# Vector products through SBUF, a third PSUM bank for background work, and one GpSimd instruction for two scan results

## The chip, the core and the metric

The kernel runs on one core of a Trainium2 chip. A core has a matrix engine (TensorE: PE, its weight loads PEld), a vector engine (VectorE: DVE), a scalar engine (ScalarE: ACT), a general engine (GpSimd: POOL) and a queue processor (SyncE: SP) that here issues every DMA. Each engine runs its own instructions in their order and waits on semaphores for the others. Data lie in HBM, in SBUF (128 partitions, the working memory) and in PSUM (128 partitions of eight 2 KB banks), which the matrix engine writes.

The metric is the device time of one execution in microseconds: 11066.59 as the median of three (11065.08 to 11072.03).

## What is computed

Two layers on `x` of shape (8, 96, 64, 64). Layer 0 is a state space block (normalization, a projection, a 3x3 depthwise convolution, a selective scan in four directions, a gate) followed by a small convolutional block with channel attention; layer 1 is linear attention and an 8-bit feed-forward. Nearly all of the time is in the selective scan of layer 0:

```python
delta = softplus(dts + dt_bias)
h0 = zeros((b, K, D_INNER, D_STATE))          # K = 4 directions, 192 channels, 16 states

def step(h, inp):                             # over L = 4096 positions
    u_t, d_t, b_t, c_t = inp
    dA = exp(d_t[..., None] * A)
    h = dA * h + (d_t * u_t)[..., None] * b_t[:, :, None, :]
    y = einsum('bkdn,bkn->bkd', h, c_t)
    return (h, y)
```

For each of 8 images, 4 directions, 192 channels and 16 states a first-order recurrence runs over 4096 positions; the states are then weighted with `c_t` and summed.

## The kernel before

**Tiling of the scan.** Images go in 4 pairs `p`. The 2 x 192 channels of a pair fill three blocks `T` of 128 rows. Positions go in 4 chunks `ci` of 1024 columns. One (p, k, ci, T) is a job; there are 192 (`jobs`, before the main loop at L1400). In a job a tile of 128 partitions holds 32 channels x 4 states; `j` counts the four groups of channels and `q` the four groups of states. One (job, j, q) is a unit of 128 x 1024 numbers, 3072 in all. The main loop takes two units a turn, so it has 1536 pairs.

**One pair, by engine.**
- PE: `spread(g)` (L1299) copies 32 rows of `du` (delta times input) to 128 partitions, into the PSUM tile `pu` (2 banks), once for every four units (a group `g`).
- ACT: `decay(u)` (L1304) makes `da` = exp(A delta) in SBUF, four buffers.
- VectorE: `scan(u)` (L1311). First two products `pb[i]` = `pu` x `bm` (`bm` is B of the recurrence, loaded in SBUF); then two scans `hc` = scan(`da`, `pb[i]`), which start from `carry` but in the first chunk. In this text the products are P0 and P1, the scans S0 and S1, in this order. Both `pbs` are PSUM tiles of two banks each (L437); `hc` is in SBUF, 8 buffers of one unit (L426).
- GpSimd: in the same function, for each of the two units, a copy of the last column into `carry` (not in the last chunk, `ci` = 3) and the product `hc` = `hc` x `cm` (`cm` is C of the recurrence). Its four instructions stand in the order copy, product, copy, product, each copy waiting for its own scan.
- PE and ACT: `total(g-1)` (L1349) sums four units of the group before over states into the PSUM tile `yp`; ACT copies the sum to `y` and SP stores it, some with a read-back of the sum of another direction (`prev`, `yet`).
- SP: `weights` (L1268) loads `bm` and `cm` ahead (4 and 5 buffers), `fetch` loads `dl`. A `cm` or `bm` tile belongs to a (q, batch) and is used for two or four `j`.

**Order on the engines.** `pe`, `ve`, `se`, `ge` are recorders of the class `InOrder` (L254): each engine's instructions are chained in the order in which the program writes them, so every one of them has line 266 in the profile. A tile scheduler orders only the DMAs by their own waits.

**Background work.** All that isn't the scan (the convolutions and projections of the next pair of images, the gate and the second block of the last one, `du` and `dls` of the next job through `steps`, L467) is written as Python generators, "lanes", that a planner of class `Slots` (L283) steps twice a pair: `slots.run()` once before `scan(u)` and once after it. A lane that needs PSUM calls `take` (L301): it gets bank `pg` on even slots or `yp` on odd ones (`yp` is also `total`'s) where the bank is free and where two running budgets of PE and ACT time, filled at RATE a slot up to CAP, are positive; `long` asks hold `pg` over several slots. `give` (L321) frees a bank one slot later. PSUM is full: `pg` 1 + `yp` 1 + `pu` 2 + two `pbs` 4 = 8 banks. Background work on GpSimd (products `u`, `du`, `turn`, `acc`, `tn`) stands between the `hc` products in its order.

After the loop a tail (`tp`, `tps` pools) finishes the last pair of images; ahead of it phase A does the first.

Of the kernel before, what the change touches and what calls it, by code (L numbers as in the profile page):

```python
# [9 lines left out]
F32 = mybir.dt.float32  # L10
F16 = mybir.dt.float16
BF16 = mybir.dt.bfloat16
F8 = mybir.dt.float8e5
AF = mybir.ActivationFunctionType
ALU = mybir.AluOpType
# [4 lines left out]
B, C, H, W = 8, 96, 64, 64  # L20
# [7 lines left out]
CH = 1024  # L28
NCH = L // CH
# [253 lines left out]
class Slots:  # L283
# [4 lines left out]

    RATE, CAP = (2.0, 1.8), (3.0, 2.4)

    def __init__(self, *banks):
        self.lanes, self.later, self.first, self.at, self.due = [], [], None, 0, {}
        self.banks, self.held, self.big = banks, set(), set()
        self.left, self.behind = [0.0, 0.0], lambda: False

    def pay(self, *times):
        self.left = [v - t for v, t in zip(self.left, times)]

    def take(self, pe, act, long=0):  # L301
        while True:
            i = 1 if self.at % 2 and not long else 0


            due = long and (
                self.at % 4 > (long == 2) or self.at % 16 <= 6 < self.at % 16 + long
            )
            if i not in self.held and not due and min(self.left) > (-2 if long else 0):
                self.held.add(i)  # L310
                self.pay(pe, act)
                return self.banks[i]
            yield

    def take_big(self, *which):
# [4 lines left out]

    def give(self, bank):  # L321
        i = self.banks.index(bank)
        self.after(1, lambda: self.held.remove(i))

    def after(self, n, f):
# [25 lines left out]
def phase_b(  # L351
# [7 lines left out]
    nc = tc.nc  # L359
    with ExitStack() as ctx:  # L360
# [25 lines left out]
        make_identity(nc, ident)  # L386
        eps = cp.tile([128, 1], F32, name="eps")
        nc.vector.memset(eps, EPS)
        gmean = cp.tile([C, C], F32, name="gmean")
        nc.vector.memset(gmean, 1.0 / (C * 128))  # L390
        mean96 = cp.tile([C, C], F32, name="mean96")
        nc.vector.memset(mean96, 1.0 / C)
        vec = load("vec96", [C, 10])
# [29 lines left out]
        inner = ExitStack()  # L423
        bcp = inner.enter_context(tc.tile_pool(name="b_bc", bufs=4))
        wp = inner.enter_context(tc.tile_pool(name="b_w", bufs=2))
        hp = inner.enter_context(tc.tile_pool(name="b_h", bufs=8))  # L426
        gp = inner.enter_context(tc.tile_pool(name="b_bg", bufs=1))
        psc = inner.enter_context(tc.tile_pool(name="b_ps", bufs=1, space=PSUM))

# [4 lines left out]
        yps = psc.tile([128, 512], F32, name="yp")  # L434
        bank0 = psc.tile([128, 512], F32, name="pg")
        pu = psc.tile([128, CH], F32, name="pu")
        pbs = [psc.tile([128, CH], F32, name=f"pb{i}") for i in range(2)]  # L437
        pe = InOrder(tc, nc.tensor, mybir.EngineType.PE)
        ve = InOrder(tc, nc.vector, mybir.EngineType.DVE)
        se = InOrder(tc, nc.scalar, mybir.EngineType.Activation)  # L440
        ge = InOrder(tc, nc.gpsimd, mybir.EngineType.Pool)
        halves = [slice(h * 512, h * 512 + 512) for h in range(CH // 512)]
        slots = Slots(bank0, yps)

        jobs = [
            (p, k, ci, T) for p in range(NP) for k in ((1, 3, 0, 2) if p else (0, 2, 1, 3))
            for ci in range(NCH) for T in (0, 2, 1)
        ]
        units = [(job, j, q) for job in range(len(jobs)) for j in range(4) for q in range(4)]
        carries, bcs, dus, dls, sts, das, hcs, prevs, yet = ({} for _ in range(9))  # L450
        turned, resting, squeezed_at = set(), set(), set()

        def where(job):
# [4 lines left out]
        def batch(u):  # L458
            job, j, q = units[u]
            T = jobs[job][3]  # L460
            return j // 2 if T == 2 else T
# [5 lines left out]
        def steps(job):  # L467

            p, k, ci, c, T, at = where(job)
            if T == 0:  # L470

                sts[job // 3] = gp.tile([32 + 2 * R, 512], F32, name="st")
                r0 = 64 + R * (k // 2)
                for i, hs in enumerate(halves):
                    for b in range(2):
                        nc.sync.dma_start(
                            sts[job // 3][32 * i + R * b : 32 * i + R * b + R, :],
                            xd_d[k % 2][2 * p + b][r0 : r0 + R, at][:, hs],
                        )
            dtw = gp.tile([32 + 2 * R, 128], F32, name="dtw")  # L480
            for i in range(2):
                nc.sync.dma_start(dtw[32 * i : 32 * i + 2 * R, :], a["dtw"][:, k, T, :])
            dus[job] = gp.tile([128, CH], F32, name="du", bufs=2)
            nc.sync.dma_start(dus[job], xi_d[k % 2][p][T][:, at])
            yield

            while slots.at % 16 != 6:
                yield
            dl = gp.tile([128, CH], F32, name="dls")
            for i, hs in enumerate(halves):  # L490
                bank = slots.banks[i]
                assert i not in slots.held
                slots.held.add(i)
                slots.pay(0.9, 2.5)
                rows = slice(32 * i, 32 * i + 2 * R)
                pe.matmul(bank, dtw[rows, :], sts[job // 3][rows, :], start=True, stop=True)
                se.activation(dl[:, hs], bank, AF.Softplus, bias=dtb[:, k, T : T + 1])
                slots.give(bank)
                if i:
                    exps()  # L500
                else:
                    yield
            ge.tensor_mul(dus[job], dus[job], dl)
            yield from wait(2)
            nc.sync.dma_start(dl_d[k][p][T][:, at], dl)
            yield
# [243 lines left out]
        def rest(b, s):  # L750
# [139 lines left out]
            for j in range(8):  # L890
# [14 lines left out]
                x8 = gp.tile([C, 512], F8, name=f"x8{s}")  # L905
                se.copy(x8, xc, saturate=False)
                yield
                h8 = gp.tile([128, 3, 512], F8, name=f"h8{s}")

                def cast(o, t):  # L910
                    return lambda: se.copy(o, t, saturate=False)
# [1 line left out]
                for i in range(3):  # L913
                    bank = yield from slots.take(0.3, 1.3)
                    pe.matmul(bank, w1q[:, i * 128 : i * 128 + 128], x8, start=True, stop=True)
                    h16 = gp.tile([128, 512], F16, name=f"h16{s}")
                    se.copy(h16, bank)
                    se.activation(h16, h16, AF.Relu, bias=b1f[:, i : i + 1])
                    slots.give(bank)
                    slots.after(1, cast(h8[:, i, :], h16))  # L920
                    yield
                yield from wait(1)
                bank = yield from slots.take(0.7, 1.3)
                for i in range(3):
                    pe.matmul(
                        bank[0:C, :], w2q[:, i, :], h8[:, i, :], start=(i == 0), stop=(i == 2)
                    )
                o16 = gp.tile([128, 512], F16, name=f"h16{s}")[0:C, :]
                se.copy(o16, bank[0:C, :])
                se.activation(o16, o16, AF.Identity, bias=b2f)  # L930
                slots.give(bank)
# [85 lines left out]
        def before_scans(p):  # L1017
# [26 lines left out]
            def norms(b):  # L1044
# [16 lines left out]
                for j in js:  # L1061
# [13 lines left out]
                    if j < 7:  # L1075
                        nxt = fetch(j + 1)
                    bank = yield from slots.take(0.1, 2.5)
                    pe.matmul(bank[0:C, 0:4], gmean, cs, start=True, stop=True)
                    se.mul(ngm, bank[0:C, 0:4], -1.0)
                    slots.give(bank)  # L1080
                    sq = u(5)[0:C, 0:512]
                    for i, q in enumerate(quarters):
# [3 lines left out]
                        )  # L1086
                    yield
                    bank = yield from slots.take(0.1, 0.5)
                    pe.matmul(bank[0:C, 0:4], gmean, gs, start=True, stop=True)
                    se.activation(r, bank[0:C, 0:4], AF.Ln, bias=eps[0:C])  # L1090
                    se.activation(r, r, AF.Exp, scale=-0.5)
                    slots.give(bank)
                    slots.after(1, times(ngm, r))
# [174 lines left out]
        def weights(u, i):  # L1268

            if u >= len(units):  # L1270
                return
            job, j, q = units[u]
            p, k, ci, c, T, at = where(job)
            b = batch(u)
            if (job // 3, b, q, i) in bcs:
                return
            t = bcp.tile([128, CH], F32, name=("bm", "cm")[i], bufs=(4, 5)[i])
            r0 = 32 * (k // 2) + 16 * i + 4 * q
            nc.sync.dma_start(
                t, xd_d[k % 2][2 * p + b][r0 : r0 + 4, at].unsqueeze(0).to_broadcast([32, 4, CH])  # L1280
            )
            bcs[job // 3, b, q, i] = t

# [27 lines left out]
        def scan(u):  # L1311

            job, j, q = units[u]
            p, k, ci, c, T, at = where(job)
            step, last = (-1, 0) if k >= 2 else (1, CH - 1)
            for i in range(2):
                ve.tensor_mul(pbs[i], pu, bcs[job // 3, batch(u), q + i, 0])
            for i in range(2):
                t = hp.tile([128, CH], F32, name="hc")
                carry = carries[p, k][:, T, 4 * j + q + i : 4 * j + q + i + 1]  # L1320
                ve.tensor_tensor_scan(
                    t[:, ::step], das.pop(u + i)[:, ::step], (pbs[i])[:, ::step],
                    0.0 if ci == 0 else carry, ALU.mult, ALU.add,
                )
                hcs[u + i] = t
            for i in range(2):
                v = u + i
                carry = carries[p, k][:, T, 4 * j + q + i : 4 * j + q + i + 1]
                if ci < NCH - 1:
                    ge.tensor_copy(carry, hcs[v][:, last : last + 1])  # L1330
                ge.tensor_mul(hcs[v], hcs[v], bcs[job // 3, batch(u), q + i, 1])

        def before(g):

# [14 lines left out]
        def total(g):  # L1349
# [9 lines left out]
            for n in range(4):  # L1359
                for i in range(4):  # L1360
                    pe.matmul(
                        yp[32 * i : 32 * i + 32, :], add,
                        hcs[4 * g + n][:, 256 * i : 256 * i + 256],
                        start=(n == 0 and k < 2), stop=(n == 3),
                    )
            for n in range(4):
                hcs.pop(4 * g + n)
            y = wp.tile([128, 256], F32, name="y")
            to = y_d if k == 2 else ys_d[1]
# [577 lines left out]
```

## Time and profile before

| | us |
|---|---|
| median of the runs | 11066.59 |
| the profiled execution's span | 11058.4 |
| first product of the loop starts | 214.57 |
| last scan pair of the loop (starts, lasts) | 10719.00, 4.57 |
| VectorE busy between them | 10318.6 |
| GpSimd busy between them | 8960.45 |
| ACT busy between them | 6404.01 |
| PE busy between them | 7459.47 |
| mean granted TensorE clock | 0.815 |

Other rows of the view by groups that the next sections use: GpSimd's products on 128 x 512 (`u<-u,u`, 180 of them) take 1271 ns on average, the `du` products on 128 x 1024 2358 ns, the `carry` copies 183 ns. VectorE's scans without `carry` take 2275 ns. In the tail VectorE's fused products on 96 x 512 take 742 ns with an operand in PSUM (`w<-t,c_vec,w`), 740 ns from SBUF (`v<-v,c_vec,w`) and 752 ns on 128 x 512 from SBUF (`tn<-tn,c_on,cb`).

How to read it: a line of groups has the line, the engine, the operation, output<-inputs by tile name, the shapes, the count, then busy time in us and the mean of one in ns, then the idle time of the engine just before such instructions and what ended most of it. A line of the timeline has start and duration in us; equal neighbours are merged, with xcount and their joint duration.

### The profile page before, as it was taken

The numbers are of one execution on the slowest core, as the hardware profiler recorded it, in microseconds if no ns is written. First come the engines' busy times: TensorE is split into PE (matmuls) and PEld (weight loads), VectorE is DVE, ScalarE is ACT, GpSimd is POOL, SyncE is SP. The second block draws the span as 40 slices with busy tenths as digits, with TensorE's granted clock in tenths as the row PEclk, the third lists the DMA queues.
The fourth block names the chain that finished last, engine by engine and source line by source line (L and its number), as shares of the span: only waits on it lengthen the run. The fifth ranks groups of instructions, "written<-read, shape, count | busy, mean of one in ns | idle before, by whom it ended". The sixth has DMA issues, their size and how long they took to land.

```text
span 11058.4 us, 128094 instructions
## 1 busy us (share of the span) xinstructions
PE 7887.2 (71%) x39468; PEld 3111.6 (28%) x39468; DVE 10525.7 (95%) x6651; ACT 6596.3 (60%) x9175; POOL 9028.7 (82%) x6649
## 2 busy tenths in 40 slices
PE   7755778655568887767777787776767776665778
PEld 3322333222223332223222332223322222222223
DVE  4999999999999999999999999999999999999974
ACT  2544765544567666556776656565776656665554
POOL 2788877787898888998888887899889888988860
PEclk8877888877788888878878888887878877777889
DMA  3445554454555555666545555566544555644551
GB/s 117 151 165 180 160 156 157 141 188 156 163 185 172 171 172 157 211 214 195 158 152 160 157 178 159 177 220 209 172 157 159 160 164 179 197 157 140 173 157 37
DMA packets 900188, 1834.20 MB, mean 166 GB/s; under 512 B 247965, under 2 KB 421214, under 8 KB 892462
## 3 DMA queue, kind: packets, MB, share of 16 engines
q1 hardware_dynamic: 899502, 1826.01, 52.8%
q8 instruction: 314, 5.14, 0.2%
q14 instruction: 372, 3.05, 0.1%
HBM read 1405.13 MB, written 420.42 MB: 165 GB/s over the span
## 4 chain that ended last, share of the span: by engine, by line
PE 32%; issue 29%; DVE 17%; POOL 11%; ACT 6%; DMA 4%; SPq 0%; DVEq 0%; POOLq 0%; ACTq 0%
PE pu L266 12%; PE yp L266 11%; DVE hc L266 11%; POOL hc L266 7%; PE pg L266 6%; DVE pb L266 5%; ACT u L266 2%; ACT da L266 2%; POOL u L266 2%; PE t L266 2%; PE ps L197 1%; DMA bm<-xd 1%; POOL turn L266 1%; POOL carry L266 1%; ACT L266 1%
## 5 line engine op out<-in xcount | busy, mean ns | idle before, releaser
L266 POOL TENSOR_TENSOR hc<-hc,cm 128x1024 f32<-128x1024 f32 x3072 | 7230.0, 2359 | 591.0 <-DVE hc L266 382.6
L266 DVE TENSOR_TENSOR_SCAN hc<-da,carry,pb 128x1024 f32<-128x1024 f32 x2304 | 5276.8, 2334 | 38.1 <-ACT da L266 31.5
L266 PE MATMUL pu<-du,c_sel 128*128 128x512 f32 x3072 | 2452.5, 944 | 2244.1 <-DVE pb L266 2239.6
L266 DVE TENSOR_TENSOR pb<-pu,bm 128x1024 f32<-128x1024 f32 x3072 | 3601.6, 1220 | 133.9 <-PE pu L266 105.9
L266 ACT ACTIVATE da<-dl,c_alog 128x1024 f32<-128x1024 f32 x3072 | 3352.8, 1140 | 91.4 <-DVE hc L266 73.8
L266 PEld LDWEIGHTS pu<-du,c_sel 128*128 128x128 f32 x3072 | 790.0, 281 | 3521.1 <-DVE pb L266 2784.8
L266 DVE TENSOR_TENSOR_SCAN hc<-da,pb 128x1024 f32<-128x1024 f32 x768 | 1713.1, 2275 | 38.9 <-ACT da L266 22.8
L266 ACT COPY y<-yp 128x256 f32<-128x256 f32 x768 | 284.4, 370 | 2348.9 <-PE yp L266 2198.4
L266 PE MATMUL yp<-hc,c_add 128*32 128x256 f32 x24576 | 1660.8, 416 | 22.6 <-ACT s L266 6.6
L266 PEld LDWEIGHTS yp<-hc,c_add 128*32 128x32 f32 x24576 | 768.6, 120 | 1200.1 <-issue 628.4
L266 POOL COPY carry<-hc 128x1 f32<-128x1 f32 x2304 | 422.5, 183 | 766.1 <-DVE hc L266 744.9
L266 ACT ACT_TABLE_LOAD x566 | 726.2, 1283 | 38.2 <-DMA cb<-zs 16.9
L266 ACT COPY u<-pg 128x512 f32<-128x512 f32 (+6 forms) x397 | 218.3, 550 | 712.3 <-PE pg L266 641.2
L266 POOL TENSOR_TENSOR u<-u,u 96x512 f32<-96x512 f32 (+1 forms) x426 | 537.5, 1269 | 105.9 <-ACT u L266 101.8
L266 POOL TENSOR_TENSOR du<-du,dls 128x1024 f32<-128x1024 f32 x192 | 452.7, 2358 | 91.5 <-ACT dls L266 91.1
L266 ACT COPY u<-yp 96x512 f32<-96x512 f32 (+6 forms) x347 | 188.0, 542 | 465.5 <-PE yp L266 404.5
L266 PE MATMUL pg<-ain,wmain 96*128 96x512 f32 x792 | 354.1, 599 | 0.0
L266 PE MATMUL pg<-ain,wmix 96*128 96x512 f32 x792 | 353.0, 598 | 0.0
L266 PE MATMUL yp<-prev,ident 128*128 128x256 f32 x768 | 321.9, 512 | 39.0 <-ACT u L266 27.4
L266 PEld LDWEIGHTS yp<-prev,ident 128*128 128x128 f32 x768 | 214.5, 283 | 381.8 <-issue 264.3
L266 PE MATMUL pg<-st,dtw 12*128 12x512 f32 x384 | 218.5, 649 | 49.4 <-ACT u L266 28.8
L266 PE MATMUL yp<-st,dtw 12*128 12x512 f32 x384 | 227.9, 674 | 18.3 <-ACT u L266 10.9
(340 smaller groups left out, 7030.2 us busy)
## 6 DMA issues: line engine op xcount, KB each, us to landing
dl<-dl SPq DMA_DIRECT2D x768, 512.0 KB
bm<-xd SPq DMA_DIRECT2D x512, 512.0 KB
cm<-xd SPq DMA_DIRECT2D x512, 512.0 KB
du<-xi SPq DMA_DIRECT2D x192, 512.0 KB
dl<-dls SPq DMA_DIRECT2D x192, 512.0 KB
ya<-y SPq DMA_DIRECT2D x384, 128.0 KB
prev<-ya SPq DMA_DIRECT2D x384, 128.0 KB
xi<-u SPq DMA_DIRECT2D x152, 256.0 KB
```

The source lines that it names most:

```text
L197: nc.tensor.matmul(bank[r, :].rearrange("p (h w) -> p h w", w=W), w[:, t if len(which) > 1 or w is wmix else 0, columns], pads[b][:, 8 * j ...
L266: op(*args, **kw)
```

## The change

1. `pbs[0]` becomes an SBUF tile; `pbs[1]` stays in PSUM. One of its two banks becomes `ph`, a bank for the lanes.
2. `hc` tiles and `cm` tiles are now two units wide (4 and 2 buffers of two units). One copy moves both carries of a pair, one GpSimd product of 128 x 2048 multiplies both units by C.
3. `Slots` has three banks. A lane takes the bank that rested longest; a `long` ask takes `ph`, else `pg`, and one at a time. RATE goes from (2.0, 1.8) to (2.2, 2.0) and CAP from (3.0, 2.4) to (4.0, 4.0).
4. `gmean` goes (`mean96` with a scale of 1/128 in the ACT instruction that follows), `h8` and `h16` share `u` tiles, and the scratch for descriptors that software makes is set to 1024.

```diff
-    RATE, CAP = (2.0, 1.8), (3.0, 2.4)
+    RATE, CAP = (2.2, 2.0), (4.0, 4.0)
...
+    def rested(self, i):
+        return i not in self.held and self.at > self.used[i] + 1
+    def hold(self, i):
+        self.held.add(i)
+        self.used[i] = self.at
     def take(self, pe, act, long=0):
         while True:
-            i = 1 if self.at % 2 and not long else 0
-            due = long and (
-                self.at % 4 > (long == 2) or self.at % 16 <= 6 < self.at % 16 + long
-            )
-            if i not in self.held and not due and min(self.left) > (-2 if long else 0):
-                self.held.add(i)
-                self.pay(pe, act)
-                return self.banks[i]
+            at = self.at % 16
+            if long:
+                if self.at % 4 <= (long == 2) and not self.long and min(self.left) > -2:
+                    for i in (2, 0):
+                        if i not in self.held and not (i == 0 and at <= 6 < at + long):
+                            self.hold(i)
+                            self.long = i + 1
+                            self.pay(pe, act)
+                            return self.banks[i]
+            elif min(self.left) > 0:
+                free = [i for i in range(3) if self.rested(i) and not (i == 1 and at % 4 == 0)]
+                if free:
+                    i = min(free, key=lambda i: self.used[i])
+                    self.hold(i)
+                    self.pay(pe, act)
+                    return self.banks[i]
             yield
...
-        hp = inner.enter_context(tc.tile_pool(name="b_h", bufs=8))
+        hp = inner.enter_context(tc.tile_pool(name="b_h", bufs=4))
...
-        pbs = [psc.tile([128, CH], F32, name=f"pb{i}") for i in range(2)]
+        bank2 = psc.tile([128, 512], F32, name="ph")
+        pbs = [wp.tile([128, CH], F32, name="pb0", bufs=1), psc.tile([128, CH], F32, name="pb1")]
...
-        slots = Slots(bank0, yps)
+        slots = Slots(bank0, yps, bank2)
...
-            t = bcp.tile([128, CH], F32, name=("bm", "cm")[i], bufs=(4, 5)[i])
+            if i == 0:
+                t = to = bcp.tile([128, CH], F32, name="bm")
+            else:
+                if q % 2 == 0:
+                    pairs[job // 3, b, q] = bcp.tile([128, 2, CH], F32, name="cm", bufs=2)
+                t = pairs[job // 3, b, q - q % 2]
+                to = t[:, q % 2, :]
...
+            t = hcs[u] = hp.tile([128, 2, CH], F32, name="hc")
+            n = 4 * j + q
+            carry = carries[p, k][:, T, n : n + 2]
+            def product(i, to):
+                ve.tensor_mul(pbs[to], pu, bcs[job // 3, batch(u), q + i, 0])
+            product(0, 0)
+            product(1, 1)
             for i in range(2):
-                ve.tensor_mul(pbs[i], pu, bcs[job // 3, batch(u), q + i, 0])
-            for i in range(2):
-                t = hp.tile([128, CH], F32, name="hc")
-                carry = carries[p, k][:, T, 4 * j + q + i : 4 * j + q + i + 1]
                 ve.tensor_tensor_scan(
-                    t[:, ::step], das.pop(u + i)[:, ::step], (pbs[i])[:, ::step],
-                    0.0 if ci == 0 else carry, ALU.mult, ALU.add,
+                    t[:, i, ::step], das.pop(u + i)[:, ::step], pbs[i][:, ::step],
+                    0.0 if ci == 0 else carry[:, i : i + 1], ALU.mult, ALU.add,
                 )
-                hcs[u + i] = t
-            for i in range(2):
-                v = u + i
-                carry = carries[p, k][:, T, 4 * j + q + i : 4 * j + q + i + 1]
-                if ci < NCH - 1:
-                    ge.tensor_copy(carry, hcs[v][:, last : last + 1])
-                ge.tensor_mul(hcs[v], hcs[v], bcs[job // 3, batch(u), q + i, 1])
+            if ci < NCH - 1:
+                ge.tensor_copy(carry, t[:, :, last])
+            ge.tensor_mul(t, t, bcs[job // 3, batch(u), q, 1])
...
-                    pe.matmul(bank[0:C, 0:4], gmean, cs, start=True, stop=True)
-                    se.mul(ngm, bank[0:C, 0:4], -1.0)
+                    pe.matmul(bank[0:C, 0:4], mean96, cs, start=True, stop=True)
+                    se.mul(ngm, bank[0:C, 0:4], -1.0 / 128)
...
-    nc = bacc.Bacc("TRN2", target_bir_lowering=False, num_devices=1)
+    nc = bacc.Bacc(
+        "TRN2", target_bir_lowering=False, num_devices=1, dynamic_dma_scratch_size=1024
+    )
```

## What I predicted, and why

> **What bounds the kernel now.** I read the page's busy shares, then its costliest groups, then the timeline of a quiet stretch.
>
> ```profile
> PE 7887.2 (71%) x39468; PEld 3111.6 (28%) x39468; DVE 10525.7 (95%) x6651; ACT 6596.3 (60%) x9175; POOL 9028.7 (82%) x6649
> ...
> L266 POOL TENSOR_TENSOR hc<-hc,cm 128x1024 f32<-128x1024 f32 x3072 | 7230.0, 2359 | 591.0 <-DVE hc L266 382.6
> L266 DVE TENSOR_TENSOR_SCAN hc<-da,carry,pb 128x1024 f32<-128x1024 f32 x2304 | 5276.8, 2334 | 38.1 <-ACT da L266 31.5
> ...
> L266 DVE TENSOR_TENSOR pb<-pu,bm 128x1024 f32<-128x1024 f32 x3072 | 3601.6, 1220 | 133.9 <-PE pu L266 105.9
> ```
>
> VectorE works 95% of the span with products (P0, P1) and scans (S0, S1) of 1536 pairs; GpSimd is second at 82%. The loop runs from the first product (214.57) to the last scan's end (10719.00 + 4.57): 10,509.0 us, 6.84 a pair. The rest of the span, 549.4 us, with the 8.2 us that the median of the runs (11,066.6) has over the profiled span (11,058.4), makes 557.6, which the change hardly touches.
>
> The timeline of the loop, VectorE and then GpSimd (start, duration):
>
> ```profile
> 228.72 4.45 DVE L266 TENSOR_TENSOR_SCAN hc<-da,pb 128x1024 f32<-128x1024 f32 x2
> 233.09 2.34 DVE L266 TENSOR_TENSOR pb<-pu,bm 128x1024 f32<-128x1024 f32 x2
> ```
>
> ```profile
> 231.06 0.18 POOL L266 COPY carry<-hc 128x1 f32<-128x1 f32 x1 [1.35 <-DVE hc L266]
> 231.33 2.34 POOL L266 TENSOR_TENSOR hc<-hc,cm 128x1024 f32<-128x1024 f32 x1
> ```
>
> GpSimd follows a scan by 0.07 to 0.1 us (10600.74 behind a scan ending at 10600.65), its product follows the carry copy's start by 0.27, and both engines run at full pace over each other. Here every VectorE instruction has at most one large SBUF operand: pu and pb lie in PSUM.
>
> Where VectorE has two SBUF operands, the ramp shows something else (first VectorE, then GpSimd):
>
> ```profile
> 18.46 0.17 DVE L134 TENSOR_TENSOR s<-r 128x9 f32<-128x9 f32 x1
> ...
> 18.71 1.51 DVE L135 TENSOR_TENSOR s<-s,tmv 128x9 f32<-128x9 f32 x1
> ...
> 26.03 1.48 DVE L134 TENSOR_TENSOR s<-r 128x8 f32<-128x8 f32 x1
> ```
>
> ```profile
> 18.57 1.63 POOL L147 TENSOR_TENSOR xt<-xt,r 128x864 f32<-128x864 f32 x1 [1.97 <-DVE st L119]
> ...
> 26.02 1.47 POOL L146 TENSOR_TENSOR xt<-xt,m 128x768 f32<-128x768 f32 x1 [4.15 <-issue]
> 27.57 1.49 POOL L147 TENSOR_TENSOR xt<-xt,r 128x768 f32<-128x768 f32 x1
> ```
>
> Nine elements take 0.17 us alone and 1.51 under a GpSimd product, ending at 20.22 as that ends at 20.20; eight end at 27.51 after 27.49. VectorE waits for the whole GpSimd instruction. At 27.49 the waiting VectorE instruction went ahead of GpSimd's next.
>
> **The change, part by part.** *Even products in SBUF.* S0 now reads da and pb0 from SBUF: 1536 scans of the kind just shown, beside an engine busy 82% of the time. P0, P1 and S1 keep one SBUF input.
>
> [...]
>
> *One GpSimd product for a pair (M).* Rows give 1.271 us for 512 columns and 2.359 for 1024, so 2048 take 2.359 + 2 x 1.088 = 4.54 (at most 2 x 2.359 = 4.72). It waits for S1, where the first of two products could start after S0. One carry copy (3 pairs in 4) replaces two; I take its 0.26.
>
> *The chain this makes.* From S1's end: 0.09 to GpSimd, 0.75 x 0.26 for the copy, 4.54 for M. P0 and P1 end 2.25 after S1 and S0 then waits for M. A blocked 768-column product (103.97, 1.73) ended 0.81 behind GpSimd's end against 0.94 unblocked, so release comes 0.13 early: S0 costs 2.33 - 0.13 = 2.20, S1 2.24 (4.57 - 2.33). Sum: 2.20 + 2.24 + 0.09 + 0.195 + 4.54 = 9.265 us a pair instead of 6.84, 14,231 for 1536. Call this "in step". Behind the waiting S0 stand S1 and the next products on VectorE; for these wait the next M, ACT's exponentials (the da buffers) and, every second pair, PE's new pu. All of them come later by as much as VectorE does and have the longer pair to catch up in, so nothing more is added.
>
> Other GpSimd work stands between two M's and has from S0's end to S1's end, 2.33. In the built order 869 of 1536 gaps hold none; at the rows' durations they sum to 1,467, and 373 gaps pass 2.33 by 251 us together. In step throughout: 14,231 + 251 + 558 = 15,040.
>
> *The other order.* If a gap's work passes about 4.2 us (2.33 plus most of the products), S0 goes first and M runs one pair behind, under S1, P0, P1 (4.41 us). Then the two only queue for each other: 1536 x (2.20 + 0.195 + 4.54) = 10,652, plus 1,467 is 12,119, with 558 is 12,677. 45 gaps lead in. A VectorE wait of over some 0.4 us leads out, since M then gets ahead again; before has 118 such waits in its loop (for pu 45, da 43, bm 19, yp 6, others 5, by the view of waits), perhaps half of them large enough. If entries and exits fall evenly, the share one behind is 45/(45 + 118) = 0.28 to 45/(45 + 59) = 0.43; I take 0.35: 15,040 - 0.35 x 2,363 = 14,213.
>
> *Banks.* For the same operation on 96x512, the row with a PSUM operand (w<-t,c_vec,w) has 742 ns and those from SBUF 740 and 752, so P0 and S0 change by -10 to +10 ns each: -31 to +31 us over 2 x 1536, 0 taken.
>
> [...]
>
> *Slots: third bank, higher rates, freer choice.* Neither kernel's planner adds an empty slot in the loop. After it the changed one needs 5 slots instead of 9. The stretch between last scan and tail is 16.5 us (10723.6 to 10740.1): 0 to -16, -5 taken. Inside, PE and ACT get their work in another order under a longer pair; if that cover went, a late pu or da costs VectorE what it does now, 106 and 54 us.
>
> *Buffers and queue.* cm keeps 4 units instead of 5, so its load waits on SP for M of the pair before, with bm and dl queued behind. Next use is about 14 us later, and the longest load wait of VectorE is 5.2: 0; at most today's 21 to 25 again. hc keeps its 8 units. The smaller descriptor scratch: the page's DMA is hardware queues alone; 0, up to today's load waits. Shared tiles and gmean change no count that matters: 0.
>
> Total 14,208, said as 14,200.
>
> **The rivals.** *No exclusion for scans* (0.09), the other side. Then 11,067, -31 to +31 for operands, -16 to 0 at the end, say 11,045. For: the blocked rows are products, none a scan. Against: a scan reads two SBUF streams like them. It decides if S0's mean stays near 2.33.
>
> *Finer sharing* (0.12). [...]
>
> *GpSimd goes first* (0.06). If its next instruction beats the waiting S0, other work lengthens each chain too: 14,231 + 1,467 + 558 = 16,256. Against: 27.49 above.
>
> **How the numbers follow.** Whole-instruction exclusion has 0.73 and spans 12,600 (all one behind) to 15,320 (in step, M at 4.72). Adding most of finer sharing puts the low end at 11,700; about 2 in 10 is left out. What a measurement can tell is about 0.2%. Only the first rival is not slower: 0.06 faster, 0.03 same; slower 0.91.
>
> **What would show it.** VectorE's busy share stays high but the scan group's mean rises from 2334 ns to some 3000 to 3600, since a blocked scan counts as busy; in step alternate scans last near 4.9 us and end 2.2 after an M. GpSimd falls below 65% busy in step, and its M lasts about 4.54. A pair takes 9.1 to 9.4 in step, 7 to 8 one behind. It is wrong if S0 keeps 2.33 under a running M; the share is wrong if one order holds throughout.

## The result, and the profile after

| | before | after |
|---|---|---|
| median of the runs, us | 11066.63 | 14590.88 |
| profiled span | 11058.4 | 14594.8 |
| loop, first product to last scan | 10509.0 | 14042.2 |
| a pair of units | 6.842 | 9.142 |
| VectorE busy in the loop | 10318.6 | 13752.1 |
| mean of S0, of S1 | 2.328, 2.311 | 4.555, 2.300 |

The ratio is 1.318 (95% interval 1.3165 to 1.3202). Outside the loop the span holds 552.5 us against 549.4, so all of the loss is in the loop. There VectorE is busy 3,433 us more and idle 100 us more (290.2 against 190.4), and the mean of S0 alone makes (4.555 - 2.328) x 1536 = 3,421. The means are counted from the starts and ends in the traces, S0 being every first scan of a pair. The granted TensorE clock fell too, from 0.815 to 0.744, but VectorE waited no longer for PE's `pu` (105.9 us before, 100.9 after), so a late PE isn't what costs.

From the page after, the busy shares and groups:

```profile
PE 8306.8 (57%) x39468; PEld 3246.6 (22%) x39468; DVE 13958.7 (96%) x6650; ACT 6734.1 (46%) x9232; POOL 10079.7 (69%) x3961
...
L266 DVE TENSOR_TENSOR_SCAN hc<-da,carry,pb 128x1024 f32<-128x1024 f32 x2304 | 7759.6, 3406 | 152.3 <-ACT da L266 128.4
L266 POOL TENSOR_TENSOR hc<-hc,cm 128x2048 f32<-128x2048 f32 x1536 | 6965.1, 4535 | 1279.4 <-DVE hc L266 1024.8
...
L266 DVE TENSOR_TENSOR pb<-pu,bm 128x1024 f32<-128x1024 f32 x3072 | 3582.2, 1204 | 124.1 <-PE pu L266 100.9
...
L266 POOL TENSOR_TENSOR du<-du,dls 128x1024 f32<-128x1024 f32 x192 | 729.7, 3800 | 62.3 <-ACT dls L266 62.2
```

VectorE's share even rises, from 95 to 96%: a scan that waits inside the engine counts as busy. What gives it away is the mean, 3406 ns instead of 2334, for the same shape. The wide GpSimd product takes 4535 ns, while a `du` product of unchanged shape goes from 2358 to 3800: GpSimd waits too.

The timeline of a quiet stretch after, VectorE (start, duration; the last line is one scan, cut by the window):

```profile
7040.66 7.05 DVE L266 TENSOR_TENSOR_SCAN hc<-da,carry,pb 128x1024 f32<-128x1024 f32 x2
7047.64 2.33 DVE L266 TENSOR_TENSOR pb<-pu,bm 128x1024 f32<-128x1024 f32 x2
...
7056.87 2.33 DVE L266 TENSOR_TENSOR pb<-pu,bm 128x1024 f32<-128x1024 f32 x2
7059.11 4.82 DVE L266 TENSOR_TENSOR_SCAN hc<-da,carry,pb 128x1024 f32<-128x1024 f32 x1
```

and GpSimd in the same stretch:

```profile
7038.82 4.51 POOL L266 TENSOR_TENSOR hc<-hc,cm 128x2048 f32<-128x2048 f32 x1
7043.29 4.36 POOL L266 TENSOR_TENSOR du<-du,dls 128x1024 f32<-128x1024 f32 x1
...
7057.01 0.18 POOL L266 COPY carry<-hc 128x2 f32<-128x2 f32 x1 [4.45 <-DVE hc L266]
7057.27 4.51 POOL L266 TENSOR_TENSOR hc<-hc,cm 128x2048 f32<-128x2048 f32 x1
```

The pair repeats after 7056.87 - 7047.64 = 9.23 us. S0 is issued at 7059.11 while M runs from 7057.27 to 7061.78, and ends at 7063.93, 2.15 behind M. Two pairs earlier, `du` was issued as M ended (7043.33) and took 4.36 instead of 2.36: S0 went first, and GpSimd waited 2 us for it.

The other order, M one pair behind, is there too. GpSimd and then VectorE:

```profile
3919.95 2.19 POOL L266 COPY carry<-hc 128x2 f32<-128x2 f32 x1
3922.23 4.50 POOL L266 TENSOR_TENSOR hc<-hc,cm 128x2048 f32<-128x2048 f32 x1
3926.69 3.25 POOL L266 TENSOR_TENSOR u<-u,u 96x512 f32<-96x512 f32 x1
```

```profile
3919.24 5.11 DVE L266 TENSOR_TENSOR_SCAN hc<-da,pb 128x1024 f32<-128x1024 f32 x2
3924.27 2.33 DVE L266 TENSOR_TENSOR pb<-pu,bm 128x1024 f32<-128x1024 f32 x2
3926.52 4.54 DVE L266 TENSOR_TENSOR_SCAN hc<-da,pb 128x1024 f32<-128x1024 f32 x2
...
3955.74 2.57 DVE L266 TENSOR_TENSOR pb<-pu,bm 128x1024 f32<-128x1024 f32 x2 [7.05 <-DMA bm<-xd]
```

Here other GpSimd work ran long, S0, issued at 3919.24, got in behind it, and the 0.18 us copy took 2.19. M then ran under S1 and the next products, and the next S0 (3926.52) hardly waited. At 3955.74 a late load held VectorE, M caught up, and the loop was in step again. Counted over the trace by which ends first, S0 or the M of the pair before, 1313 pairs are in step, at 9.37 us from one S0's end to the next, and 222 one behind, at 7.79.

S0 does not always go ahead of GpSimd's next instruction. Of the cases in the loop where it had waited 0.3 us or more and GpSimd's next followed at once, S0 went first in 610 of 621. The longest S0, of 10.03 us from 9800.61 on, let three more GpSimd instructions pass, after the M that ran at its start:

```profile
9798.34 4.52 POOL L266 TENSOR_TENSOR hc<-hc,cm 128x2048 f32<-128x2048 f32 x1
9802.81 1.18 POOL L266 COPY u<-big 128x256 f32<-128x256 f32 x2
9803.95 4.54 POOL L266 TENSOR_TENSOR hc<-hc,cm 128x2048 f32<-128x2048 f32 x1
```

What decides the order in such cases was not tried.

### The profile page after: what moved, and what is told of

Its sections match the earlier page's. It is cut to its first block, busy times and chain, and to the rows that moved or that the text cites. A ratio compares the mean times of both kernels' runs of the same rounds, so it can differ in the third digit from the quotient of the medians.

```text
span 14594.8 us, 122970 instructions
## 1 busy us (share of the span) xinstructions
PE 8306.8 (57%) x39468; PEld 3246.6 (22%) x39468; DVE 13958.7 (96%) x6650; ACT 6734.1 (46%) x9232; POOL 10079.7 (69%) x3961
## 4 chain that ended last, share of the span: by engine, by line
issue 54%; POOL 15%; DVE 14%; PE 11%; DMA 3%; ACT 3%; SPq 0%; POOLq 0%; DVEq 0%; ACTq 0%
DVE hc L266 10%; POOL hc L266 8%; PE pu L266 3%; PE yp L266 3%; DVE pb L266 3%; POOL u L266 3%; PE ph L266 2%; POOL turn L266 1%; PE t L266 1%; ACT u L266 1%; POOL carry L266 1%; PE pg L266 1%; POOL du L266 1%; ACT da L266 1%; PE ps L197 1%
## 5 line engine op out<-in xcount | busy, mean ns | idle before, releaser
L266 DVE TENSOR_TENSOR_SCAN hc<-da,carry,pb 128x1024 f32<-128x1024 f32 x2304 | 7759.6, 3406 | 152.3 <-ACT da L266 128.4
L266 POOL TENSOR_TENSOR hc<-hc,cm 128x2048 f32<-128x2048 f32 x1536 | 6965.1, 4535 | 1279.4 <-DVE hc L266 1024.8
L266 PE MATMUL pu<-du,c_sel 128*128 128x512 f32 x3072 | 2669.7, 1020 | 5091.7 <-DVE pb L266 5087.8
L266 DVE TENSOR_TENSOR pb<-pu,bm 128x1024 f32<-128x1024 f32 x3072 | 3582.2, 1204 | 124.1 <-PE pu L266 100.9
L266 DVE TENSOR_TENSOR_SCAN hc<-da,pb 128x1024 f32<-128x1024 f32 x768 | 2651.3, 3491 | 33.9 <-ACT da L266 33.9
L266 POOL COPY carry<-hc 128x2 f32<-128x2 f32 x1152 | 417.3, 362 | 2696.8 <-DVE hc L266 2605.4
L266 POOL TENSOR_TENSOR u<-u,u 96x512 f32<-96x512 f32 (+1 forms) x474 | 1091.4, 2310 | 10.8 <-ACT u L266 7.1
L266 POOL TENSOR_TENSOR du<-du,dls 128x1024 f32<-128x1024 f32 x192 | 729.7, 3800 | 62.3 <-ACT dls L266 62.2
L266 PE MATMUL ph<-ain,wmain 96*128 96x512 f32 x684 | 339.9, 642 | 42.0 <-ACT u L266 33.2
L266 PE MATMUL ph<-ain,wmix 96*128 96x512 f32 x720 | 329.8, 604 | 0.0
L266 POOL TENSOR_TENSOR turn<-turn,big 128x256 f32<-128x256 f32 x192 | 275.0, 1451 | 3.5 <-ACT turn L266 3.5
```

The lines of the kernel that those rows point to most:

```text
L266: op(*args, **kw)
```

## The experiments

Each run has its own runs of the kernel before beside it (medians 11062 to 11066). The theory: a scan with two SBUF inputs and GpSimd's copies and products, which read SBUF, exclude each other for a whole instruction (S0 at 4.56 us against 2.33). S0 and S1 name the first and second unit's scans, as above.

### Both products in PSUM

```diff
-        pbs = [wp.tile([128, CH], F32, name="pb0", bufs=1), psc.tile([128, CH], F32, name="pb1")]
+        pbs = [psc.tile([128, CH], F32, name=f"pb{i}") for i in range(2)]
...
-        slots = Slots(bank0, yps, bank2)
+        slots = Slots(bank0, yps)
```

(and the class `Slots` of before.) Expected:

> The changed kernel with both products in PSUM again and so two banks and the planner of before; the GpSimd instruction for two units, the wide tiles and the small scratch stay. Theory (a scan with two SBUF inputs and a reading GpSimd instruction exclude each other): the whole loss goes, S0 falls from 4.56 to 2.33 us, time 11,020 to 11,110. Rival (the wide GpSimd instruction starts behind the second scan and holds buffers longer, so it is the cost): S0 2.33 but VectorE idle, 11,400 or more.

Measured 11076.53 us, a ratio of 1.0012 (1.0003 to 1.0021). Groups of its page:

```profile
L266 POOL TENSOR_TENSOR hc<-hc,cm 128x2048 f32<-128x2048 f32 x1536 | 6963.3, 4534 | 682.2 <-DVE hc L266 430.1
L266 DVE TENSOR_TENSOR_SCAN hc<-da,carry,pb 128x1024 f32<-128x1024 f32 x2304 | 5269.0, 2327 | 50.2 <-ACT da L266 32.0
```

The wide product still takes 4.53 us behind S1, and the scans are at 2327 ns again. So the wide instruction, the wide tiles, the shared tiles and the small scratch cost 0.1% together, and all else lies in the SBUF product and in the planner with its third bank.

### Only the product in SBUF

The kernel before with this one edit, and the small scratch for room:

```diff
-        pbs = [psc.tile([128, CH], F32, name=f"pb{i}") for i in range(2)]
+        pbs = [wp.tile([128, CH], F32, name="pb0", bufs=1), psc.tile([128, CH], F32, name="pb1")]
```

> The kernel before with one edit: pb0 in SBUF (and the small scratch that makes room). Two GpSimd products a pair, two banks, planner of before. Theory: GpSimd reads and S0 queue for one port: 1536 x (2.20 + 0.39 + 4.63) + 1,467 + 558 = 13,115, so 12,700 to 13,400, S0 near 3.4 to 3.9 us. Rival (the third bank, the planner or the wide GpSimd instruction cost the time): 11,067 within 1%, S0 2.33.

Measured 12802.63, ratio 1.157 (1.155 to 1.159); S0's mean 3.12, S1's 2.30. One tile's place costs 1,737 us, with the planner, banks and GpSimd instructions of before. The "one port" of the expectation is its author's picture: no run shows a port, only that S0 waits, 0.79 us on average here (3.12 against 2.33). S0 is under the expected 3.4, but the time lies in the range, since VectorE also idles more before its products and scans, 711 us against 211, for late `da` and `pu` above all. From its page:

```profile
L266 DVE TENSOR_TENSOR_SCAN hc<-da,carry,pb 128x1024 f32<-128x1024 f32 x2304 | 6182.1, 2722 | 303.6 <-ACT da L266 263.8
...
L266 DVE TENSOR_TENSOR pb<-pu,bm 128x1024 f32<-128x1024 f32 x3072 | 3586.4, 1206 | 305.8 <-PE pu L266 196.3
```

### Even exponentials in PSUM, the product still in SBUF

```diff
-        bank2 = psc.tile([128, 512], F32, name="ph")
+        da0 = psc.tile([128, CH], F32, name="da0")
...
-            das[u] = wp.tile([128, CH], F32, name="da", bufs=4)
+            das[u] = wp.tile([128, CH], F32, name="da", bufs=2) if u % 2 else da0
```

(two banks and the planner of before.)

> pb0 stays in SBUF, but the other large input of the same scan, the even da, is a PSUM tile (one buffer, in the banks that the third bank and pb0 left; two banks and the planner of before for the lanes). VectorE writes the product to SBUF as in the change, and each scan has one SBUF input. Theory: no exclusion, S0 2.33, 10,990 to 11,180. Rival (VectorE's writes of the product to SBUF, or any SBUF read of pb0, collide with GpSimd): S0 stays above 3.5 us, 13,000 or more.

Measured 11078.51, ratio 1.0012 (1.0003 to 1.0021).

```profile
L266 DVE TENSOR_TENSOR_SCAN hc<-da,carry,pb 128x1024 f32<-128x1024 f32 x2304 | 5280.9, 2336 | 59.9 <-ACT da L266 38.7
```

Here `pb0` is in SBUF as in the change, VectorE writes and reads it there, and the loss is gone, because the scan's other input came from PSUM. It is the second SBUF input of the scan that costs (the row above has 2336 ns, in the change 3406). What matters among GpSimd's operands was not tried.

### Without the products with C

```diff
-            ge.tensor_mul(t, t, bcs[job // 3, batch(u), q, 1])
```

> The changed kernel without the GpSimd products with C (the states are summed unweighted); the carry copies and the other GpSimd work stay. Theory: S0 waits only under that other work, 1,467 us in all: S0's mean 2.35 to 2.6, 10,900 to 11,350. Rival (a scan with both inputs in SBUF is slow by itself): S0 near 4.5 us, 14,000 or more.

Measured in one run: 11385.94; S0's mean 2.42.

```profile
L266 DVE TENSOR_TENSOR_SCAN hc<-da,carry,pb 128x1024 f32<-128x1024 f32 x2304 | 5372.8, 2373 | 123.4 <-ACT da L266 104.2
```

The scan with both inputs in SBUF is not slow by itself; it waits for GpSimd (4.56 us beside these products). The time is 36 us over the range, which pointed at something else: VectorE's waits, from the view of waits of this run,

```profile
DVE pb L266 <- PE pu L266: 204.9, 105, 20.1
DVE hc L266 <- ACT da L266: 149.8, 86, 7.2
```

(us in total, times, longest), where the kernel with both products in PSUM has 103.3 and 50.3.

### The same with the planner of before

```diff
-        slots = Slots(bank0, yps, bank2)
+        slots = Slots(bank0, yps)
```

> The run without the products with C again, with the planner of before and its two banks (pb0 still in SBUF); the products with C are left out here too. The run with the third bank took 11,386, S0's waits make some 150 us of what it has over a VectorE-bound 11,070, and waits for pu and da are 170 us longer than with both products in PSUM. Theory (the third bank's planner bunches PE and ACT work, so pu and da come late): 11,180 to 11,260. Rival (those waits come from S0's blocking alone): 11,386 within 0.5%.

Measured 11084.33, ratio 1.0017 (1.0006 to 1.0027), and

```profile
DVE pb L266 <- PE pu L266: 46.5, 31, 20.1
...
DVE hc L266 <- ACT da L266: 29.1, 28, 5.0
```

S0's mean is 2.41, as with the third bank, so the 302 us between the two kernels are the planner's: waits for `pu` and `da` go from 76 to 355 us. The time lies below the 11,180 to 11,260 that the theory here expected: the planner's part is larger than it had, and S0's 0.09 us of waiting a pair cost little net. Which part of the planner does it, the third bank, the choice or the higher rates, was not tried.

### GpSimd's work split as before

```diff
-            if ci < NCH - 1:
-                ge.tensor_copy(carry, t[:, :, last])
-            ge.tensor_mul(t, t, bcs[job // 3, batch(u), q, 1])
+            for i in range(2):
+                if ci < NCH - 1:
+                    ge.tensor_copy(carry[:, i : i + 1], t[:, i, last : last + 1])
+                ge.tensor_mul(t[:, i, :], t[:, i, :], bcs[job // 3, batch(u), q, 1][:, i, :])
```

> The changed kernel with the GpSimd work of a pair split again into copy, product, copy, product. Theory: as for pb0 in SBUF alone, 12,700 to 13,400, so the wide instruction costs about 1,500 of the 3,500 us because it makes S1, M and S0 one chain; the difference from that run, below 150 us, is the planner's. Rival (the wide instruction only saves GpSimd overhead): 14,600 or more.

Measured 12920.92, ratio 1.168 (1.166 to 1.170); S0's mean 3.05. Two short instructions instead of a long one take back 1,670 of the 3,524 us, although GpSimd then has more instructions. The 118 us over the run with the product in SBUF alone are the planner's and the wide tiles' together.

### Two halves, both behind S1

```diff
-            ge.tensor_mul(t, t, bcs[job // 3, batch(u), q, 1])
+            for i in (1, 0):
+                ge.tensor_mul(t[:, i, :], t[:, i, :], bcs[job // 3, batch(u), q, 1][:, i, :])
```

> The changed kernel with M as two products of one unit, both behind the copy and so behind S1 as M was (the second unit's first). The same work from the same point, 0.25 us more a pair. Theory (S0 waits for the one GpSimd instruction that runs, and goes ahead of the next): S0 starts behind the first half, the second runs under S1; a pair takes 7.1 us plus the other GpSimd work, 0.95: 12,370 + 558 = 12,930, so 12,600 to 13,100, S0's mean near 3. Rival (S0 waits until GpSimd's queue of ready work is empty): 14,590 or more, S0 above 4.5.

Measured 12778.24, ratio 1.155 (1.153 to 1.157); S0's mean 2.99.

```profile
L266 POOL TENSOR_TENSOR hc<-hc,cm 128x1024 f32<-128x1024 f32 x3072 | 8947.9, 2934 | 338.5 <-DVE hc L266 185.6
L266 DVE TENSOR_TENSOR_SCAN hc<-da,carry,pb 128x1024 f32<-128x1024 f32 x2304 | 6110.2, 2691 | 400.9 <-ACT da L266 307.9
```

The work starts where M started, and one cut in it takes back 1,813 us. S0 waits for the instruction that runs and mostly goes ahead of the next, whose mean grows from 2.36 to 2.93 by the wait. Counted as above, S0 went first in 1143 of 1178 cases. The gain of the split is thus the shorter instruction and not the earlier start of its first half.

### The PSUM scan first

```diff
-            for i in range(2):
+            for i in (1, 0):
                 ve.tensor_tensor_scan(
```

> The changed kernel with the two scans of a pair in the other order: the one from PSUM first, then the one from SBUF. Theory: M then runs under P0, P1 and the PSUM scan (4.41 us) and a pair takes 6.9 us and the other GpSimd work, 0.95, in full: 12,070 + 558 = 12,630, so 12,400 to 13,000; the SBUF scan's mean falls from 4.56 to about 3. Rival (each SBUF scan under GpSimd simply runs slower, wherever it stands): 14,600.

Measured 12780.06, ratio 1.155 (1.153 to 1.157). The SBUF scan, now last, has a mean of 2.98, the first 2.33 (both stand in one row of its page):

```profile
L266 DVE TENSOR_TENSOR_SCAN hc<-da,carry,pb 128x1024 f32<-128x1024 f32 x2304 | 6066.5, 2675 | 298.5 <-ACT da L266 135.1
```

M runs under the products and the PSUM scan; not one instruction is added or taken away, and 1,811 us come back. The order decides how much of the exclusion shows.

## Why the prediction came out as it did

- **Exclusion of S0 and GpSimd's copies and products, whole instructions: right.** Of S0's operands the second SBUF input matters (11,079 with `da` in PSUM), the wait is for the instruction that runs (S0's mean 4.56 with M whole, 2.99 with the two halves), and S0 as a rule goes ahead of GpSimd's next (`du` at 7043.29; 610 of 621 cases). The prediction had it so from the one place at 27.49, without the exceptions. None of the three rivals held: S0 did not stay near 2.33, in step it ended 2.15 us behind M's end, of 2.34 that it takes by itself, and so shared next to nothing with it, and GpSimd's next went first in only 11 of those 621 cases. The range's low end, 11,700, counts on a sharing that no run shows: with it S0 would have ended less than those 2.15 us behind M.
- **That GpSimd waits as well** was assumed, without a row for it, in two terms of the sum: the 2.33 us that other work has from S0's end to S1's, and the 12,677 of the order in which the two queue for each other. It is shown now: 2.36 to 4.36 us for a `du` product. Before shows it too: in the ramp a GpSimd product that takes 1.32 us at 184.60 took 1.85 when it came 0.23 us behind a VectorE product with two SBUF inputs (first VectorE, then GpSimd):

```profile
177.07 0.91 DVE L145 TENSOR_TENSOR xn<-xn,s 128x768 f32<-128x768 f32 x1
```

```profile
177.30 1.85 POOL L147 TENSOR_TENSOR xt<-xt,r 128x672 f32<-128x672 f32 x1 [1.74 <-DVE r L132]
...
184.60 1.32 POOL L147 TENSOR_TENSOR xt<-xt,r 128x672 f32<-128x672 f32 x1
```

- **The chain in step: right.** 9.07 (no carry copy) to 9.33 us was the sum, quiet stretches have 9.17 and 9.23. M was 4.535 against 4.54. With other GpSimd work a pair in step took 9.37 against (14,231 + 251)/1536 = 9.43. S0 ended 2.15 us behind M (the median) where 2.20 was taken from a single blocked product; over 1313 pairs that is 66 us.
- **One behind: right as a mechanism, 7.79 us against 7.89 ((12,677 - 558)/1536).**
- **The share one behind was mis-sized, 0.35 against 222/1535 = 0.145.** Its term, 0.35 x 2,363 = 827 us, should have been 342; with that the sum is 14,693. There were 26 entries instead of 45. The long gaps are there as counted: 24 of the 45 led in, but 11 met a loop that was one behind already, and 10 did not lead in. A stay lasted 8.5 pairs, not the 13 to 26 that 118 or 59 exits in 1536 pairs amount to. Of the 26 exits 22 fall on a VectorE wait of over 0.3 us. The step that failed is "if entries and exits fall evenly": such a wait follows 52 of the 222 pairs one behind and 26 of the 1312 in step. Why the waits gather there was not tried; the pair is shorter there and covers less, and the stretches with much background work that lead in may also be those with late loads.
- **Banks: right.** P0 went from 1.213 to 1.193 us, 31 us in all and at the edge of the -31 to +31 given for P0 and S0. P1, whose tile stayed in PSUM, went from 1.227 to 1.216, another 17 us. S0 from SBUF saved nothing: in the run without the products with C under the old planner its median, with carry, is 2.341 us, before 2.340.
- **Slots at -5 us: wrong, but covered for the most part.** I argued that a different order inside is harmless under a longer pair and gave the price without the cover as today's waits, 106 and 54. Without it the planner costs 302 us, most of it in waits for `pu` and `da`; in the change VectorE's waits for them are 101 and 162. The step looked for empty slots and for the end, and not for when PE and ACT deliver. At the end nothing was saved either: the stretch from the last scan to the tail is 16.6 us (14256.4 to 14273.0), as before.
- **A sign that missed:** GpSimd was to be under 65% busy in step and was 68%, counted over the pairs in step. Its own waits count as busy too: a `du` product takes 3800 ns on average where it took 2358.

From its sum of 14,208 the prediction missed 14,591 by 383 us: 485 from the share, less 80 from the pairs in step (0.06 x 1313, of which S0's early release is 66), less 22 from those one behind (0.10 x 222).

## What to carry to other kernels

Before moving an operand of a VectorE instruction from PSUM to SBUF, count its SBUF inputs. Here two of them tied a scan to GpSimd's copies and products, and S0 went from 2.33 to 4.56 us: the price was what was left of the GpSimd instruction that ran, at times of the next as well (11 of 621 cases). Where that can't be avoided, keep GpSimd's instructions short (M in two halves: 1,813 of the 3,524 us back) and put the two-input one where GpSimd has little left to do (the PSUM scan first: 1,811 back). A freed bank for background work promised little here, where VectorE waited only 160 us for `pu` and `da`; with the planner that used it, it cost 302 us without the products with C.

## What the runs showed of the hardware

- A blocked VectorE instruction is inside its busy time: the page shows 96% VectorE, of which 3,421 us are waiting. The mean against the same shape elsewhere shows it (S0 4.555 us against 2.328).
- The smallest GpSimd copies wait as well: a 128x2 copy of 0.18 us took up to 2.26, while S0 ran.
- Of two that wait for each other VectorE's scan mostly went first, but not always: GpSimd's next instruction passed it in 11 of 621 cases in the change and in 35 of 1178 with two halves.
- With GpSimd's large products left out, a scan with two SBUF inputs waited only 0.09 us on average (S0 2.42 and 2.41 us against 2.33), with GpSimd busy 17% of the span.
- No version tried beats the kernel before, in which VectorE's own work is 6.72 us (10,318.6/1536) of the 6.84 of a pair; those with the planner of before in which S0 hardly waits are at a ratio of 1.0012 to 1.0017.
